# One decoder layer on one core: the order of the product stream worked out from product and wait lengths, with three groups' keys and values moved beside the first chain

## The chip, the cores and the metric

One core of a Trainium2 chip runs the whole layer in one launch. The metric is the time of an execution in microseconds of device time; the median of 3 runs of the kernel before is 2039.08 us (2031.9 to 2040.92).

## What is computed

The input x is 64 sequences of 128 tokens with 256 channels, the context ctx has the same shape, all in 32-bit floats. Cut to what matters:

```
x = layernorm(x + mamba(x))                  # xn = layernorm(x)*gamma+beta; xz = xn @ W_in (256 -> 2x512)
                                             # 4-tap causal convolution, silu, W_x -> B, C (16 each), delta
                                             # h = exp(delta*A)*h + delta*B*x ; y = h.C ; (y + D*x)*silu(z) @ W_out + x
x = layernorm(x + xattn(x, ctx))             # q = rot(x@Wq), k = rot(ctx@Wk), v = ctx@Wv ; (q k^T * decay) v, no softmax
x = layernorm(x + shared(x) + top-2 of 8 routed experts)   # silu(x@gate)*(x@up) @ down, hidden 512
```

`A` is the same for all channels here, so the kernel takes the branch `shared_decay`, which turns the recurrence into products of 128 x 128 matrices.

## The kernel before, in words

The 64 sequences are worked in 16 groups of 4 (512 tokens). A group goes through a **first half** (`front`, `scan`: layernorm, W_in, convolution, W_x, delta, the scan as products), a **second half** (`after`, `route`: W_out, layernorm, keys, values and queries, attention, layernorm, the router, and two scatters of 4 row blocks each to the expert lists in DRAM), and the **shared expert** (`shared`). Beside these run the **routed tiles**: 78 tiles of 256 or 128 rows, read from the lists, put through one expert's gate, up and down products with weights that are fetched tile by tile (1.5 MB each, three buffers), and scattered back. The tiles come in five batches; `tile_list` makes a batch's list after groups 4, 8, 12 and 16 (the last makes two).

Everything is written as Python generators that yield between steps. Each engine executes its instructions in the program's order, so the order in which the steps are recorded decides what a late operand holds up. Before, `weave` sets that order: for every yield of the first half of group g (30 are assumed) it advances the second half of group g-1 by 28/30 of a step, the shared expert of group g-2 by 8/30, and the routed tiles by 6 steps for each tile due in this tick; at the tick's end the others are run to their end. A tick is thus a border: nothing of tick g+1 stands ahead of what is left of tick g. The build then moves instructions locally on an engine where the build's own scheduling finds a gap, so the listing of the built program decides, not the source alone.

Names that the steps below use, by line of the kernel before: the normalised rows are transposed (L560, `xn` for the first half, `x` for the second), W_in makes `xc` and `sz` (L574), W_x (L630), `bcs` is transposed (L642), from it comes `dl` on VectorE and ScalarE (L673 to L694), the product of `d` (L713), 16 small products into `pof` (L724), `eb`, `bj`, `cj` (L729 to L731) and their product (L746), transposes of `xc` (L756), the product with `mt` (L763), W_out (L583), attention products (L837, L850), the router's `logit` (L909) and `sel` (L942). PSUM has 5 buffers `pm` and 3 `gu`; `cT`, the transposed context of one group, has one buffer and is loaded from the POOL queue. `one` is a pool of single buffers, so `sz` of the next group may be written only after W_out has read it.

After the 16 groups the rest of the tiles run with the shared expert of group 15 (L583/L574 on `gu`), then the shared experts of groups 7 to 13 beside the final sums (`combine`, L1208), layernorms and stores.

Of the kernel before, what the change touches and what calls it, by code (L numbers as in the profile page):

```python
# [11 lines left out]
F32 = mybir.dt.float32  # L12
# [497 lines left out]
def _shared_decay(ctx, K):  # L510
# [22 lines left out]

    xts = [K.x0] + [const.tile([P, GB, D], F32, name=f"xt{i}") for i in range(2)]

    def layernorm(dst, src):
# [12 lines left out]
        yield  # L549
# [5 lines left out]
    def transposed(dst, src, scale=None, bias=None):  # L555

        for k in range(KD):
            ps = pm.tile([P, T], F32, name="pm")
            for b in range(GB):
                nc.tensor.transpose(ps[:, b * L : (b + 1) * L], src[:, b, k * P : (k + 1) * P], ident)  # L560
            if scale is None:
                nc.scalar.copy(dst[:, k, :], ps)
            else:
                nc.scalar.activation(
                    dst[:, k, :], ps, AF.Identity, bias=bias[:, k : k + 1], scale=scale[:, k : k + 1]
                )
# [4 lines left out]
    def project(ps, w, col, src):  # L571

        for k in range(KD):
            nc.tensor.matmul(  # L574
                ps, lhsT=w[:, k, col : col + P], rhs=src[:, k, :],
                start=(k == 0), stop=(k == KD - 1),
            )

    def project_rows(ps, src, w, cols):

        chunks = len(src)
        for k in range(chunks):
            nc.tensor.matmul(ps, lhsT=src[k], rhs=w[:, k, cols], start=(k == 0), stop=(k == chunks - 1))  # L583
# [6 lines left out]
    def front(st):  # L590
# [5 lines left out]
        yield  # L596
        xnT = one.tile([P, KD, T], F32, name="xnT", tag="xnT")
        transposed(xnT, xn, gam, bet)
        yield
# [3 lines left out]
        for c in range(CI):  # L603
# [12 lines left out]
            yield  # L616
        nc.scalar.activation(xcf, xcf, AF.Silu)
        sz = one.tile([P, CI, T], F32, name="sz")
        for c in range(CI):
# [3 lines left out]
            yield  # L623
# [4 lines left out]
        for c in range(CI):  # L628
            for h in range(2):
                nc.tensor.matmul(  # L630
# [8 lines left out]
        yield  # L639
        ptk = pm.tile([P, 2, 2, 64], F32, name="pm")  # L640
        for j in range(2):
            nc.tensor.transpose(  # L642
# [26 lines left out]
        yield  # L669
# [7 lines left out]
        yield  # L677
# [11 lines left out]
        yield  # L689
# [5 lines left out]
        yield  # L695
        st.update(xcf=xcf, sz=sz, dl=dl, tok=tok, bj=bj, cj=cj, cq=cq)

    def scan(st):
# [11 lines left out]
        yield  # L710
        yield
        pin = pm.tile([P, GB, Q], F32, name="pm")
        nc.tensor.matmul(pin.rearrange("p b i -> p (b i)"), lhsT=after_in, rhs=d1.rearrange("p b i -> p (b i)"), start=True, stop=True)  # L713
# [5 lines left out]
        nc.scalar.activation(eq, eq, AF.Exp)  # L719
        yield  # L720
        pof = pm.tile([KB, T], F32, name="pm")
        for b in range(GB):
            for q in range(4):
                nc.tensor.matmul(  # L724
# [4 lines left out]
        nc.scalar.activation(eb, pof, AF.Exp, scale=a_col)  # L729
        nc.vector.tensor_tensor(bj, bj, eb, ALU.mult)  # L730
        nc.vector.tensor_tensor(cj, cj, eb, ALU.mult)  # L731
        yield
# [11 lines left out]
        pmt = pm.tile([P, GB, L], F32, name="pm")  # L744
        for b in range(GB):
            nc.tensor.matmul(  # L746
                pmt[:, b, :], lhsT=bj[:, b * L : (b + 1) * L], rhs=cj[:, b * L : (b + 1) * L], start=True, stop=True
            )
# [4 lines left out]
        for b in range(GB):  # L753
            ps = pm.tile([P, DI], F32, name="pm")
            for c in range(CI):
                nc.tensor.transpose(ps[:, c * P : (c + 1) * P], xcf[:, c, b * L : (b + 1) * L], ident)  # L756
            nc.scalar.activation(xd[b // 2][:, b % 2, :], ps, AF.Copy, scale=dl[:, b : b + 1])
            yield
        acc = st["sz"]
        for c in range(CI):  # L760
            ps = pm.tile([P, GB, L], F32, name="pm")
            for b in range(GB):
                nc.tensor.matmul(  # L763
# [7 lines left out]
            yield  # L771
        st["acc"] = acc

    def after(g, st):
# [3 lines left out]
        cT = one.tile([P, KD, T], F32, name="cT", tag="cT")  # L778
        nc.gpsimd.dma_start(
            out=cT, in_=ctxT[:, g * T : (g + 1) * T].rearrange("(k p) t -> p k t", p=P)  # L780
        )
# [12 lines left out]
        yield  # L794
        yield from layernorm(x1, x1)
        yield
        x1T = one.tile([P, KD, T], F32, name="x1T")
        transposed(x1T, x1)
        yield

        def rotated(w, src, table, name, tag):

            ev = pm.tile([P, T], F32, name="pm")
            od = pm.tile([P, T], F32, name="pm")
            project(ev, w, 0, src)
            project(od, w, P, src)
            cos = rot_s[:, table, :].unsqueeze(1).to_broadcast([P, GB, L])
            sin = rot_s[:, table + 1, :].unsqueeze(1).to_broadcast([P, GB, L])
            r = one.tile([P, 2, T], F32, name=name, tag=tag)
            r0, r1 = seqs(r[:, 0, :]), seqs(r[:, 1, :])  # L810
            tmp = one.tile([P, GB, L], F32, name="tmp", tag="tmp")
            nc.vector.tensor_tensor(r0, seqs(ev), cos, ALU.mult)
            nc.vector.tensor_tensor(tmp, seqs(od), sin, ALU.mult)
            nc.vector.tensor_tensor(r0, r0, tmp, ALU.subtract)
            nc.vector.tensor_tensor(r1, seqs(od), cos, ALU.mult)
            nc.vector.tensor_tensor(tmp, seqs(ev), sin, ALU.mult)
            nc.vector.tensor_tensor(r1, r1, tmp, ALU.add)
            return r

        kh = rotated(wk_s, cT, 2, "kh", "kh")  # L820
        yield
        v = one.tile([P, GB, D], F32, name="v")
        for j in range(GB // 2):
            ps = pm.tile([P, 2, D], F32, name="pm")
            for i in range(2):
                b = 2 * j + i
                project_rows(
                    ps[:, i, :], [cT[:, k, b * L : (b + 1) * L] for k in range(KD)], wv_s, slice(0, D)
                )
            nc.scalar.copy(v[:, 2 * j : 2 * j + 2, :], ps)  # L830
        yield
        qh = rotated(wq_s, x1T, 0, "qh", "qh")
        yield
        pss = pm.tile([P, GB, L], F32, name="pm")
        for b in range(GB):
            for half in range(2):
                nc.tensor.matmul(  # L837
# [6 lines left out]
        yield  # L844
        x2 = x1
        for j in range(GB // 2):
            ps = pm.tile([P, 2, D], F32, name="pm")
            for i in range(2):
                b = 2 * j + i
                nc.tensor.matmul(ps[:, i, :], lhsT=sc[:, b, :], rhs=v[:, b, :], start=True, stop=True)  # L850
# [3 lines left out]
        yield  # L854
# [36 lines left out]
    def route(g, st):  # L891
# [3 lines left out]
        yield  # L895
# [3 lines left out]
        for k in range(KD):  # L899
            for b in range(GB):  # L900
                nc.tensor.matmul(
# [5 lines left out]
        yield  # L907
        pr = pm.tile([P, GB, 32], F32, name="pm")
        nc.tensor.transpose(pr.rearrange("p b e -> p (b e)"), logit, ident)  # L909
# [3 lines left out]
        yield  # L913
# [24 lines left out]
        yield  # L938
        yield
        pc = pm.tile([P, GB, NE], F32, name="pm")  # L940
        pcf = pc.rearrange("p b e -> p (b e)")
        nc.tensor.matmul(pcf, lhsT=upto, rhs=sel.rearrange("p b e -> p (b e)"), start=True, stop=False)  # L942
        nc.tensor.matmul(pcf, lhsT=ones, rhs=pre.rearrange("p b e -> p (b e)"), start=False, stop=True)
        yield
# [26 lines left out]
        yield  # L971
# [7 lines left out]
        yield  # L979
# [5 lines left out]
    def shared(x2, x2T, x2s):  # L985
# [5 lines left out]
        for c in range(CF):  # L991
# [8 lines left out]
            yield  # L1000
# [20 lines left out]
    def tile_list(k):  # L1021
# [7 lines left out]
        nc.tensor.matmul(pn, lhsT=ones, rhs=count, start=True, stop=True)  # L1029
# [52 lines left out]
    def fill_behind():  # L1082


        for j in range(2 * NE - 1):
# [13 lines left out]
            yield  # L1099
# [3 lines left out]
    def refill():  # L1103

        while fetched[0] < min(room[0], known[0]):
            ahead.append(fetch(fetched[0]))
            fetched[0] += 1

    fetched = [0]
# [25 lines left out]
    def routed():  # L1135

        def hidden(i, t):
            _, size = shape(i)  # L1140
            w = weights[i % NW]
            wg = w[:, 0:SZ].rearrange("p (k i) -> p k i", k=KD)
            wu = w[:, SZ : 2 * SZ].rearrange("p (k i) -> p k i", k=KD)
            ps = pm.tile([P, KD, size], F32, name="pm")
            for k in range(KD):
                for j in range(size // P):
                    nc.tensor.transpose(ps[:, k, j * P : (j + 1) * P], t[:, j, k * P : (k + 1) * P], ident)  # L1147
            tT = tiles.tile([P, KD, size], F32, name="rows_T", bufs=2)
            nc.scalar.copy(tT, ps)
            to = tiles.tile([P, size // P], mybir.dt.int32, name="to", bufs=3)  # L1150
            nc.gpsimd.tensor_copy(to, t[:, :, D])
            wt = tiles.tile([P, size // P], F32, name="wt", bufs=3)
            nc.gpsimd.tensor_copy(wt, t[:, :, D + 1])
            yield
            hid = []
            each = T // size
            for c0 in range(0, CF, each):
                psg = gu.tile([P, each, size], F32, name="gu")
                psu = gu.tile([P, each, size], F32, name="gu")
                for ps, w2 in ((psg, wg), (psu, wu)):  # L1160
                    for c in range(each):
                        project(ps[:, c, :], w2, (c0 + c) * P, tT)
                    yield
                hc = tiles.tile([P, each, size], F32, name="hid", bufs=4)
                nc.scalar.activation(hc, psg, AF.Silu)  # L1165
                nc.vector.tensor_tensor(hc, hc, psu, ALU.mult)  # L1166
                hid += [hc[:, c, :] for c in range(each)]
            return hid, to, wt

        def down(i, hid, to, wt):  # L1170
            _, size = shape(i)
            wd = weights[i % NW][:, 2 * SZ :].rearrange("p (c h) -> p c h", c=CF)
            ps = pm.tile([P, size // P, D], F32, name="pm")
            y = tiles.tile([P, size // P, D], F32, name="rows_out", bufs=2)
            for j in range(size // P):
                project_rows(ps[:, j, :], [h[:, j * P : (j + 1) * P] for h in hid], wd, slice(0, D))
            for j in range(size // P):
                nc.scalar.activation(y[:, j, :], ps[:, j, :], AF.Copy, scale=wt[:, j : j + 1])  # L1178
                s = nc.gpsimd.indirect_dma_start(  # L1179
                    out=ys, in_=y[:, j, :], in_offset=None,  # L1180
# [408 lines left out]
```

## Time and profile before

| what | value |
|---|---|
| median of 3 runs | 2039.08 us |
| the profiled execution, its own time | 2045.25 us |
| its span, first to last instruction | 2043.5 us |
| TensorE matmul busy, instructions | 1897.4 us, 9252 |
| VectorE, ScalarE, GpSimd busy | 985.8, 775.4, 459.6 us |
| mean DMA rate | 124 GB/s |
| mean granted TensorE clock | 0.984 |
| `ACT_TABLE_LOAD` in the trace | 110, 1.283 us each |

How to read it: a product of 32-bit floats stands in the trace as two matmul instructions, a transpose as one. Busy time of TensorE is the union of the instructions from their start to their modelled end, so short pauses between pipelined products do not show as idle time. "A <- B" with a number is time in which the engine stood idle, and the instruction that ended the wait. The windows give the busy time of each engine in a stretch of the span.

### The profile page before, as it was taken

What the parts mean: (1) busy time and instruction counts of PE and PEld (TensorE: products, weight loads), DVE (VectorE), ACT (ScalarE), POOL (GpSimd) and SP (SyncE); (2) the same over time, 40 slices, a digit from 0 to 9 for tenths busy, and PEclk for the clock granted to TensorE, in tenths of its full rate; (3) what the DMA queues carried; (4) which work ended last, traced back from release to release, by engine and by line L of the source; (5) the groups of instructions that cost most, each with busy time, mean ns of one, the idle gap of its engine ahead of it and who ended that gap; (6) DMA issues with size and microseconds to landing.
All of it is one profiled execution on the core that took longest, in us unless ns stands there. A gap on an engine that the chain in (4) does not pass through costs nothing.

```text
span 2043.5 us, 26128 instructions
## 1 busy us (share of the span) xinstructions
PE 1897.4 (93%) x9252; PEld 1389.6 (68%) x9252; DVE 985.8 (48%) x2398; ACT 775.4 (38%) x1261; POOL 459.6 (22%) x697
## 2 busy tenths in 40 slices
PE   4899999899999999999998999999989999999997
PEld 2655666575767676777676777777767888887554
DVE  3666676555666546454545454554431111112573
ACT  3365355244443435353535353525222122221331
POOL 3021221130312122222223131313132122221110
PEclk9899999999999999999999999999999999999998
DMA  4111121431422234243434343424244455853772
GB/s 145 27 54 44 42 64 52 147 96 35 132 70 87 90 130 136 84 139 120 138 114 139 105 147 111 124 96 164 88 136 170 145 203 178 312 200 114 247 274 68
DMA packets 100628, 253.59 MB, mean 124 GB/s; under 512 B 22824, under 2 KB 60328, under 8 KB 91528
## 3 DMA queue, kind: packets, MB, share of 16 engines
q1 hardware_dynamic: 77368, 196.56, 29.7%
q0 software_dynamic: 17616, 52.46, 7.4%
q10 hardware_dynamic: 5504, 2.81, 0.5%
q8 instruction: 75, 1.23, 0.2%
q14 instruction: 65, 0.53, 0.1%
HBM read 207.33 MB, written 58.60 MB: 130 GB/s over the span
## 4 chain that ended last, share of the span: by engine, by line
PE 71%; DVE 10%; DMA 6%; ACT 5%; issue 3%; POOL 2%; another core or an unknown queue 1%; SPq 0%; DVEq 0%; ACTq 0%; POOLq 0%
PE gu L574 25%; PE pm L583 17%; PE pm L574 14%; PE gu L583 4%; PE pm L763 3%; DMA cq<-chunks 2%; DMA routed_w<-in_ffn_dram 2%; PE pm L560 2%; PE pm L837 1%; PE pm L756 1%; DVE st L541 1%; POOL rstd L546 1%; PE pm L850 1%; PE pm L1147 1%; DVE gq L738 1%
## 5 line engine op out<-in xcount | busy, mean ns | idle before, releaser
L574 PE MATMUL gu<-rows_T,routed_w 128*128 128x256 f32 (+1 forms) x2496 | 511.8, 355 | 12.1 <-DMA routed_w<-in_ffn_dram 5.8
L574 PEld LDWEIGHTS gu<-rows_T,routed_w 128*128 128x128 f32 x2496 | 416.4, 191 | 77.0 <-issue 27.7
L583 PE MATMUL pm<-routed_w,hid 128*128 128x256 f32 x1080 | 251.5, 381 | 9.9 <-DVE hid L1166 9.9
L1166 DVE TENSOR_TENSOR hid<-hid,gu 128x512 f32<-128x512 f32 x135 | 92.5, 685 | 327.7 <-PE gu L574 306.4
L574 PE MATMUL pm<-xnT,w_in_s 128*128 128x512 f32 x512 | 242.9, 598 | 1.8 <-DVE halfT L1302 1.1
L574 PE MATMUL gu<-x2T,shared_w 128*128 128x512 f32 x512 | 233.4, 601 | 0.9 <-DVE hc L998 0.9
L583 PEld LDWEIGHTS pm<-routed_w,hid 128*128 128x128 f32 x1080 | 200.7, 190 | 44.5 <-DVE hid L1166 14.7
L1179 POOL DMA_INDIRECT ys<-rows_out,to x135 | 134.9, 999 | 345.7 <-ACT rows_out L1178 304.0
L1165 ACT ACTIVATE hid<-gu 128x512 f32<-128x512 f32 x135 | 80.5, 596 | 239.2 <-PE gu L574 203.4
L574 PEld LDWEIGHTS gu<-x2T,shared_w 128*128 128x128 f32 x512 | 95.3, 191 | 108.9 <-issue 101.5
L612 DVE SCALAR_TENSOR_TENSOR xc<-pm,cw,xc 128x508 f32<-128x508 f32 (+2 forms) x192 | 140.2, 740 | 58.4 <-ACT xc L607 55.4
L1178 ACT ACTIVATE rows_out<-pm,wt 128x256 f32<-128x256 f32 x135 | 57.8, 471 | 272.4 <-PE pm L583 240.6
L574 PEld LDWEIGHTS pm<-xnT,w_in_s 128*128 128x128 f32 x512 | 95.5, 192 | 83.1 <-issue 71.0
L546 POOL TENSOR_TENSOR rstd<-var,mhalf 128x4 f32<-128x4 f32 x64 | 69.2, 1081 | 325.8 <-DVE var L544 174.5
L583 PE MATMUL gu<-shared_w,hc 128*128 128x256 f32 x512 | 125.1, 394 | 14.5 <-DVE hc L998 7.8
L583 PEld LDWEIGHTS gu<-shared_w,hc 128*128 128x128 f32 x512 | 97.2, 196 | 36.0 <-DVE hc L998 12.8
L583 PE MATMUL pm<-w_out_s,sz 128*128 128x256 f32 x512 | 115.2, 380 | 1.8 <-DVE xc L767 1.0
L583 PEld LDWEIGHTS pm<-w_out_s,sz 128*128 128x128 f32 x512 | 96.1, 190 | 16.3 <-DVE sz L770 2.1
L767 DVE SCALAR_TENSOR_TENSOR xc<-xc,dsk,pm 128x512 f32<-128x512 f32 x64 | 46.9, 743 | 114.6 <-PE pm L763 51.7
L551 ACT ACTIVATE x<-x,shift,rstd 128x256 f32<-128x256 f32 x136 | 73.3, 592 | 58.2 <-DVE shift L548 58.2
L607 ACT ACTIVATE xc<-pm,cb,cw 128x512 f32<-128x512 f32 x64 | 49.5, 774 | 115.8 <-PE pm L574 115.8
L974 POOL DMA_INDIRECT xs<-x,index x64 | 65.2, 1019 | 122.7 <-issue 41.9
(234 smaller groups left out, 2499.9 us busy)
## 6 DMA issues: line engine op xcount, KB each, us to landing
routed_w<-in_ffn_dram SPq DMA_DIRECT2D x78, 1536.0 KB
picked<-ys SPq DMA_DIRECT2D x16, 1024.0 KB
rows_in<-xs SPq DMA_DIRECT2D x57, 258.0 KB
cT<-in_ctxT_dram POOLq DMA_DIRECT2D x16, 512.0 KB
cq<-chunks SPq DMA_DIRECT2D x16, 512.0 KB
x_rows<-x SPq DMA_DIRECT2D x16, 512.0 KB
xt<-in_x_dram POOLq DMA_DIRECT2D x10, 512.0 KB
xt<-x_rows SPq DMA_DIRECT2D x10, 512.0 KB
```

The lines of the kernel that those rows point to most:

```text
L546: nc.gpsimd.tensor_tensor(rstd, var, mhalf, ALU.pow)
L551: nc.scalar.activation(dst[:, b, :], src[:, b, :], AF.Identity, bias=shift[:, b : b + 1], scale=rstd[:, b : b + 1])
L574: nc.tensor.matmul(ps, lhsT=w[:, k, col : col + P], rhs=src[:, k, :], start=(k == 0), stop=(k == KD - 1),)
L583: nc.tensor.matmul(ps, lhsT=src[k], rhs=w[:, k, cols], start=(k == 0), stop=(k == chunks - 1))
L607: nc.scalar.activation(xcf[:, c, :], ps, AF.Identity, bias=cb[:, c : c + 1], scale=cw[:, c, TAPS - 1 : TAPS],)
L612: nc.vector.scalar_tensor_tensor(xc[:, c, :, s:], ps3[:, :, : L - s], cw[:, c, TAPS - 1 - s : TAPS - s], xc[:, c, :, s:], ALU.mult, ALU.add,)
L763: nc.tensor.matmul(ps[:, b, :], lhsT=xd[b // 2][:, b % 2, c * P : (c + 1) * P], rhs=mtf[:, b, :], start=True, stop=True)
L974: s = nc.gpsimd.indirect_dma_start(out=xs, in_=rows[k][:, b, :], in_offset=None, out_offset=bass.IndirectOffsetOnAxis(ap=index[:, b, k : k ...
L1165: nc.scalar.activation(hc, psg, AF.Silu)
L1166: nc.vector.tensor_tensor(hc, hc, psu, ALU.mult)
L1178: nc.scalar.activation(y[:, j, :], ps[:, j, :], AF.Copy, scale=wt[:, j : j + 1])
L1179: s = nc.gpsimd.indirect_dma_start(out=ys, in_=y[:, j, :], in_offset=None, out_offset=bass.IndirectOffsetOnAxis(ap=to[:, j : j + 1], axis=0),)
```

## The change

The generators now yield numbers. `product` and `turn` wrap each matmul and transpose and add an assumed length to a running count `work`; a yield's number is the assumed time until the chain's next product has its operands. `abreast` takes the place of `weave`: of the chains whose wait is over by `work`, it advances the one that is least far along; if none is ready, it sets `work` forward. `placed` gives each chain its place: group number plus the share of an assumed length (54 for a first half, 60 for a second, 23 for a shared expert, 11 for a tile).

```diff
+    def product(out, lhsT, rhs, **how):
...
+        work[0] += 2 * max(0.00084 * n, 0.11 if n > 64 else 0.06) / tiled
+        nc.tensor.matmul(out, lhsT=lhsT, rhs=rhs, **how)
...
-    def weave(main, steps, *others):
...
+    def abreast(*chains):
+        alive = [[gen, whole, 0.0, 0.0] for gen, whole in chains]
+        while any(c[1] for c in alive):
+            able = [c for c in alive if c[3] <= work[0]]
+            if not able:
+                work[0] = min(c[3] for c in alive)
+                continue
+            c = min(able, key=lambda c: c[2])
+            try:
+                c[2], wait = next(c[0])
...
+            c[3] = work[0] + wait
```

The borders between ticks go: first halves, second halves, shared experts and tiles are four chains that run through all groups, each held only by what it needs (`read`, `scanned`, `routed`, `added`; the tiles by a list and by 12.0 of assumed time after a fetch).

Keys and values leave `after` and become `keys`; for groups 0, 1 and 2 a fifth chain `early_keys` makes them at the start, those of groups 1 and 2 in weight buffers of the tiles that are not yet in use. Their context is loaded from the SP queue, not POOL's:

```diff
+    def early_keys(places):
+        for g, place in enumerate(places):
+            cT = load_context(g, nc.sync)
+            yield 10.0 if g == 0 else 4.0
+            yield from keys(states[g], cT, place)
...
+    abreast(
+        (placed(early_keys([None] + weights[1:]), 0.0, 40.0), True), (first_halves(), True), (second_halves(), True), (shared_ones(), True), (tiles_beside(), True),
+    )
```

From group 3 on, the keys are made while the layernorm after W_out runs, before the transposes of `x1`. In `scan`, the products into `pof` stand ahead of `eq`'s exponent, `eb`'s exponent ahead of it too, and the product of `bj` and `cj` ahead of the operations on `eq`. The two scatters of 4 rows each in `route` get a yield of 5.0 after each. `down` of a tile yields between its row blocks. After the groups, `other_tiles`, `fill_behind` and the shared expert of group 15 run under `abreast`, then the late shared experts and the sums. No arithmetic changes.

## Prediction
> **What bounds the kernel now.** I read the busy times first, then the windows tick by tick, then TensorE's waits, then the timeline. The page's first part and its clock:
>
> ```profile
> PE 1897.4 (93%) x9252; PEld 1389.6 (68%) x9252; DVE 985.8 (48%) x2398; ACT 775.4 (38%) x1261; POOL 459.6 (22%) x697
> ...
> PEclk9899999999999999999999999999999999999998
> ```
>
> TensorE is the only engine near full. The change removes no product: the listing of both programs by engine (it has no times) holds the same 5106 products and transposes. So it can win only what TensorE loses between them, and 93% hides part of that. In dense stretches one instruction starts 0.429 us after the last for 128x512, 0.216 for 128x256, 0.112 for 128x128, 0.109 for a transpose; a product is two of these. Summed over the listing that is 1817 us. The span is 2043.5, so **226 us** are lost, not the 146 that the busy row leaves.
>
> Where: I cut the span at the first W_out product of each group (66.0, 139, 211.2 us ... in the timeline), one window per tick (columns: length, then busy us of PE, PEld, DVE, ACT, POOL, clock, DMA share, GB/s):
>
> ```profile
> 0.00:66.00 66.00, 34.91 (x152) 21.78 (x153) 29.07 (x82) 25.12 (x37) 17.12 (x58) 0.87 0.40 117
> 66.00:139.00 73.00, 67.25 (x310) 39.92 (x309) 49.10 (x120) 39.58 (x56) 10.52 (x11) 0.98 0.13 34
> ...
> 448.70:540.90 92.20, 91.62 (x442) 64.39 (x442) 55.75 (x128) 39.45 (x62) 21.23 (x25) 1.00 0.28 87
> ...
> 1037.60:1143.80 106.20, 96.54 (x484) 73.94 (x483) 55.61 (x146) 43.62 (x69) 25.30 (x35) 0.95 0.38 120
> 1143.80:1241.20 97.40, 93.44 (x482) 71.21 (x481) 51.69 (x123) 43.27 (x69) 25.92 (x35) 1.00 0.41 131
> ```
>
> Window length less the products' own time in it: tick 0 loses 66.0-24.1 = 41.9; ticks 1 to 4 together 33.7; 5 to 7 together 17.0; 8 and 12, in which a tile list is made, 10.7 and 15.6; the six other late ticks 46.5 (7.7 each: 98.1-90.4 and so on); from the last W_out to the last product 46; after the last product 14.6. These add to 226.
>
> What ends the waits:
>
> ```profile
> PE pm L713 <- DVE dlb L709: 16.8, 11, 2.7
> PE pm L746 <- DVE cj L731: 13.3, 8, 3.7
> PE pm L560 <- ACT xn L551: 10.7, 1, 10.7
> PE pm L583 <- DVE hid L1166: 9.9, 17, 0.6
> PE gu L583 <- DVE hc L998: 7.8, 7, 2.6
> PE pm L763 <- ACT xd L757: 7.3, 5, 5.0
> PE pm L713 <- DVE d L705: 6.6, 2, 4.9
> PE gu L583 <- DVE hid L1166: 6.2, 1, 6.2
> ```
>
> Two small chains off TensorE, the one to `dl` and the one to `cj`, make most of what recurs. That is what an order by lengths can move.
>
> **Tick 0: keys beside the first chain.** Three groups' keys and values are 3 x (4 x 0.858 + 8 x 0.432) = 20.6 us of products, and tick 0 has 41.9 us of loss, of which some 15 lie before x is normalised. They don't fit for free, since the listing puts them ahead of products that the chain waits for:
>
> ```profile
> 39.05 1.95 PE L630 MATMUL pm<-xc,w_x_s 128*64 128x256 f32 x16 [1.61 <-ACT xc L617]
> ...
> 41.47 0.44 PE L642 MATMUL pm<-ident,bcs 128*128 128x128 f32 x2 [0.47 <-ACT bcs L635]
> 41.94 0.30 DVE L646 COPY tok<-pm 128x132 f32<-128x132 f32 x1 [4.95 <-PE pm L642]
> ...
> 46.68 0.22 DVE L709 COPY dlb<-dl 128x128 f32<-128x128 f32 x1
> ```
>
> The 12 W_in products from 26.5 us on (10.3) plus group 0's 6.9 end at 43.7, where W_x started at 39.05: 4.6 late. Group 1's key products stand between W_x and `bcs`: 3.4, less the 0.6 that the copy takes anyway, 2.8. Four of its six VectorE rotations (0.69 each) stand ahead of `tok`: 2.4 after overlap. Group 2's 6.9 fill the 3.7 before `cj` and overrun by 2.7. So the first W_out comes 12.5 late, at 78.5, and 20.6 us are done: **-8**. The SP queue now holds the context loads ahead of `bcs`'s rows; the second waits until group 0's values have read the only `cT`, which is before W_x in TensorE's order, so nothing queued on SP behind it is late. Without that cover it would delay W_x's rows by a load, 2 to 4 us. POOL loses three issues of 0.7; nobody waits for it there.
>
> **Ticks 1 to 4.** The keys are gone from 1 and 2, but tick 1 then has only 50.7 us of products against a chain of about 58 (W_out 6.9, layernorm to its first block 4.0, transposes and queries, convolution 8.4 and silu 1.9 on VectorE and ScalarE, then `dl` 5, `cj` 5.6, the product with `mt` 3.6). So part of what is moved becomes idle time there. I take 33.7 to 26: **-8**.
>
> **The recurring waits, ticks 9 to 11 and 13 to 15.** I compare what a chain needs in the trace of before with the products that the listing of after leaves for it. `bcs` to `dlb`: 10.9 us in these ticks, with 8.8 of products beside it; alone, in tick 0, 5.0. VectorE did the router's `pb`, `gt`, `same` between its links; in after's listing nothing stands between them, and only two layernorm blocks (0.59 each) on ScalarE, so it needs about 6.2 and gets 7.8: -1.6 a tick. `d` to `cj`: needed 10.5 before; after it is 5.6 (tick 0) plus what ScalarE's copies add, against 5.3 of products and the 0.9 of `pof`: -1.0. `xd` -0.8, tile products that wait for an issue and PSUM -1.4. New waits: `sel` came 6.5 us of products before `cj` and now comes 6.5 to 7.8 after it, behind 9.4 us of VectorE work (eq's four operations 5.0, gt to rank 2.0, the rest): +1.7 over today's 0.5. The second layernorm's first block needs 4.8 after L850 and gets 4.1: +0.8. `logit` +0.4. Together -1.9 a tick, **-11** for six.
>
> **Ticks 5 to 7**: the first tile's rows (3.7) and weights (1.7) are waited for in 5; the 12.0 of assumed time covers that: **-5**. **Ticks 8 and 12**: TensorE stood 5.0 and 4.1 before L763, because `xd` sat on ScalarE behind a `rows_out` whose buffer waits for GpSimd, which was issuing 8 scatters. After's listing leaves 3.8 to 5.2 of products there, and both ticks show a clock below 1 (0.97 and 0.95), which comes back with the waits: **-10** of 26.3.
>
> The skill's page "TensorE: Matmul & The Clock Gate" (section "Why this matters for your kernels") says to avoid pauses over some 3 us, since the clock is then halved. The trace agrees: among these ticks only those with waits of 4 us and more show less than 0.99. By that rule the 2 us waits that I expect cost only themselves.
>
> **After the groups.** 6.2 us before L583 at 1500 go, because 16 of group 15's gate products (13.7 us) now stand where the last lists are fetched: **-6**. From the fifth tile after that to the end, the listing of TensorE is the same in both, so 40 us and the 14.6 behind the last product stay. ScalarE loads 89 tables instead of 110 (21 x 1.283 = 27 us of an engine that is 38% busy): nothing by itself, it is in the chains above.
>
> **Sum**: -8-8-11-5-10-6 = -48 on the execution of 2045.25: 1997. It lies 6.2 above the median of 2039.08, so on that scale **1991**.
>
> **Rivals.**
> (1) *The chains keep their lengths and the closer order meets them late: slower.* The place is `bcs` to `cj` in every late tick. If `dlb` still takes 10.9 and gets 7.8, and `cj` 10.5 and gets 6.2, with `sel` and the layernorm as above, a tick loses 3.1+4.3+2.5+0.8 = 10.7 and some 2 of small waits, 5 more than today; in 11 ticks +55, less the 22 of the start and the end, about +20 with some given back in ticks 8 and 12: 2058. It decides from about 2 us above my 6.2 and 5.9 in both chains. For it: those are the measured lengths. Against: the listing has VectorE's chain in one piece.
> The same page (table at its head) gives VectorE, ScalarE and GpSimd strict FIFO queues, which speaks against packing more chains: one late operation holds all behind it. The trace has such a case (`xd` behind `rows_out` above); the rule has no price.
> (2) *The waits only change places*: ticks 5 to 15 lose what they lose today, and only start and end win: -22, 2017.
> (3) *The plan holds*: no wait recurs, as ticks 6 and 7 show already (2.5 us each). Ticks 1 to 15 then lose 3 each, 45 for 123: -78, with -14 of start and end: 1947.
>
> **Numbers.** Forecast 0.45, (1) 0.17, (2) 0.26, (3) 0.12. What a measurement of this kernel tells from no change is about 0.5%, 10 us. Of the forecast all is faster; of (2), which spreads by 12 either way, 0.18 of 0.26 is faster and 0.06 the same; of (1) 0.14 is slower and 0.03 the same; with 0.01 of doubt about the rest: faster 0.75, same 0.10, slower 0.15. The range goes from (3) to the lower half of (1): 1947 to 2040.
>
> **What would show it.** First W_out at 76 to 80, second at 134 to 139; L713's waits under 5 us in all and L746's under 8; L942's waits up from 5 to 15 or more; no wait over 3 us before L763; ticks of 94 to 97 us late; TensorE's last 14 us as before. Wrong if L713 still waits 1 us and more in each tick (1), or if the first W_out comes after 85, where the early keys cost more than they carry.

## The result, and the profile after

| | before | after | ratio, 95% interval |
|---|---|---|---|
| median | 2039.08 us (17 runs, 2031.9 to 2045.65) | 2046.15 us (17 runs, 2037.98 to 2054.11) | 1.0036 (1.002 to 1.0051) |
| the profiled execution's span | 2043.5 us | 2050.0 us | |

The change gained nothing: the time is 0.4% longer, below the 0.5% that counts here, where 48 us less were forecast. A second set of runs of the same kernel gave 1.005 (1.0034 to 1.0067).

The page of the changed kernel, as of before: busy times, and the granted clock in 40 slices.

```profile
PE 1900.6 (93%) x9252; PEld 1397.3 (68%) x9252; DVE 987.6 (48%) x2398; ACT 745.7 (36%) x1240; POOL 457.6 (22%) x694
...
PEclk9999999999999999999999999999999999999998
```

ScalarE did 30 us less (89 table loads for 110), TensorE the same: none of it reached the end. Windows again from one first W_out to the next (length, then busy us of PE, PEld, DVE, ACT, POOL, clock, DMA share, GB/s):

```profile
0.00:80.30 80.30, 54.35 (x225) 32.37 (x226) 40.23 (x99) 28.08 (x43) 16.63 (x58) 0.94 0.41 116
80.30:141.20 60.90, 55.65 (x275) 33.33 (x274) 41.76 (x109) 32.51 (x49) 6.37 (x6) 0.97 0.11 28
...
449.60:539.90 90.30, 89.34 (x446) 64.88 (x445) 54.15 (x125) 38.47 (x61) 18.73 (x24) 1.00 0.27 85
...
1033.60:1124.20 90.60, 85.53 (x448) 64.91 (x448) 50.73 (x120) 39.36 (x65) 20.24 (x24) 1.00 0.28 90
1124.20:1233.90 109.70, 99.17 (x512) 76.12 (x511) 55.79 (x148) 41.51 (x69) 30.66 (x46) 1.00 0.46 157
```

The first tick is 14 us longer and the second 12 shorter, which is the early keys. Without borders the work of a late tick varies (448 matmul instructions in one of the lines above, 512 in the next), so lengths alone no longer compare. I therefore take, for every matmul instruction, the time to the next one's start less the median spacing of its kind, and add that up as the loss (without the 4.6 us ahead of the first product and the 14.6 behind the last, which are the same in both):

| loss in us | before | predicted | after |
|---|---|---|---|
| tick 0 | 36.5 | -8 | 29.8 |
| ticks 1 to 4 | 32.2 | -8 | 35.8 |
| ticks 5 to 7 | 15.6 | -5 | 12.9 |
| ticks 8 to 15 | 69.1 | -21 | 68.4 |
| from the last W_out to the last product | 44.7 | -6 | 55.1 |
| sum | 198 | -48 | 202 |

The last product ends 6.5 us later (2028.9, 2035.4): 4 of it are loss by this count. The rest is in the medians, above all that of the 32 instructions for `d` (0.131 us before, 0.205 after), which the count takes for their spacing.

What ends TensorE's waits now (in all, times, longest); `hid` L1211 (9.9) and `xn` (10.7) stand as before, `hc` rose from 8.7 to 11.3:

```profile
PE gu L543 <- ACT rows_T L1194: 16.5, 16, 3.3
PE gu L543 <- ACT hid L1210: 11.6, 7, 1.8
PE gu L543 <- DVE hc L1044: 11.3, 10, 1.9
PE gu L543 <- DMA routed_w<-in_ffn_dram: 11.2, 7, 3.6
...
PE pm L543 <- DVE sz L784: 9.7, 10, 1.9
PE pm L543 <- DVE mk L996: 9.3, 6, 3.0
...
PE pm L543 <- DVE cj L745: 5.4, 2, 3.3
PE pm L543 <- DVE dlb L725: 4.9, 3, 4.5
```

The waits that the change was to remove are gone: `dlb` 16.8 to 4.9 (4.5 of it in tick 0), `cj` 13.3 to 5.4, `d` 6.6 to 0.2, `xd` 7.3 to 0. In their place stand three that were 0.7 us or nothing, a tile's `rows_T`, its `hid` (through the `gu` buffers) and `sz` ahead of W_out, and a longer one for the router's choice (`mk`, 3.2 before).

### The profile page after: what moved, and what is told of

The parts are those of the page before. It is cut to its first block, busy times and chain, and to the rows that moved or that the text cites. A ratio compares the mean times of both kernels' runs of the same rounds, so it can differ in the third digit from the quotient of the medians.

```text
span 2050.0 us, 26104 instructions
## 1 busy us (share of the span) xinstructions
PE 1900.6 (93%) x9252; PEld 1397.3 (68%) x9252; DVE 987.6 (48%) x2398; ACT 745.7 (36%) x1240; POOL 457.6 (22%) x694
## 5 line engine op out<-in xcount | busy, mean ns | idle before, releaser
L543 PE MATMUL gu<-rows_T,routed_w 128*128 128x256 f32 (+1 forms) x2496 | 509.1, 357 | 39.8 <-ACT rows_T L1194 16.5
L1211 DVE TENSOR_TENSOR hid<-hid,gu 128x512 f32<-128x512 f32 x135 | 92.3, 686 | 388.1 <-PE gu L543 370.2
L543 PE MATMUL pm<-routed_w,hid 128*128 128x256 f32 x1080 | 258.4, 383 | 9.9 <-DVE hid L1211 9.9
L543 PE MATMUL pm<-w_out_s,sz 128*128 128x256 f32 x512 | 124.7, 396 | 10.5 <-DVE sz L784 9.7
L543 PE MATMUL gu<-shared_w,hc 128*128 128x256 f32 x512 | 116.9, 381 | 7.3 <-DVE hc L1044 7.3
L543 PEld LDWEIGHTS gu<-shared_w,hc 128*128 128x128 f32 x512 | 95.7, 190 | 28.1 <-DVE hc L1044 11.1
L781 DVE SCALAR_TENSOR_TENSOR xc<-xc,dsk,pm 128x512 f32<-128x512 f32 x64 | 47.0, 743 | 83.3 <-PE pm L543 56.1
```

The lines of the kernel that those rows point to most:

```text
L543: nc.tensor.matmul(out, lhsT=lhsT, rhs=rhs, **how)
L781: nc.vector.scalar_tensor_tensor(y, xcf[:, c, :], dsk[:, c : c + 1], ps.rearrange("p b l -> p (b l)"), ALU.mult, ALU.add)
```

## The experiments

My theory A: the assumed waits are lengths of idle engines. ScalarE and VectorE work through their queues in order and are 36% and 48% busy, so under load an operand comes 1 to 3 us later than assumed, and a closer order makes the next consumer wait. Rivals: B, the queues set the loss whatever the order; C, the loss is made at the start and in the tail; E, the late ticks have too few independent products, so a wait that is taken from one consumer comes up at another. Ratios are to the kernel before of the same set of runs, since one kernel differed by up to 1.5% between sets; the changed kernel itself has 1.0036 and 1.005. Even the ratio of one kernel moved by 0.7% between two sets (0.9951 and 1.0021, four tiles of empty rows below), so ratios of different sets compare only to about that.

**All assumed waits times 0.33, and times 2.**

```diff
-            yield at + span * min(1.0, passed / length), wait
+            yield at + span * min(1.0, passed / length), 0.33 * wait     # the other run: 2.0 * wait
```

> The changed kernel with every assumed wait cut to a third of itself, so that a chain comes back three times too early in the order. Theory A (the order follows the assumed waits, and these are lengths of idle engines, too short under load): shorter ones make each consumer wait longer, TensorE loses 3 to 6 us more in each of 15 ticks; 2046 becomes 2090 to 2130. Rival B (the waits do not matter, since the loss is set by the in-order queues of ScalarE and VectorE, whatever the order): 2036 to 2056. Rival C (the loss sits in the start and the tail): 2040 to 2055.

Measured: 1.0113 (1.0064 to 1.0162).

> The changed kernel with every assumed wait doubled. Theory A: the consumers that now wait (rows_T 16.5 us in all, hid 11.6, sz 9.7, the router's choice 9.3, x 6.6) find their data there, and independent products fill in; 25 to 35 us go, though at some places no independent product is left: 2012 to 2030. Rival B (queues set the loss): 2036 to 2056, the same waits under other names. Rival C (start and tail): 2040 to 2055.

Measured: 1.02 (1.0152 to 1.0248). So the lengths matter, against B, but a common factor is no cure, and A's numbers were missed both times: less was lost than it said in the first run, and the second went the other way. Doubled, TensorE ran out of fill in the ticks that have no tiles: 9.8 to 10.5 us for `dlb` in each of ticks 1 to 3 (33.5 in all), 19 and 23 us lost in ticks 8 and 12. The long chains' waits were not too short; which were, is the question.

**Without the early keys.**

```diff
-        (placed(early_keys([None] + weights[1:]), 0.0, 40.0), True), (first_halves(), True), ...
+        (first_halves(), True), ...
```

> The changed kernel without the early keys and values: each group's stand again in its own second half. Theory A gives the early keys what the trace shows, 20.6 us of products in a first tick that grew by 14.3: without them 2046 becomes 2050 to 2056, and the first W_out comes at 66 to 69. Rival D (the early keys cost more than they carry, since they lengthen the first chain and empty ticks 1 to 4 of products): 2030 to 2042, with ticks 1 to 4 losing 25 us and less in place of 36.

Measured: 1.0023 (1.0 to 1.0045), not to be told from the changed kernel. The first W_out comes at 67.3 in place of 80.3, the fourth at 278.6 in place of 280.9. Tick 0 loses 37.5 (29.8 with the keys), ticks 1 to 4 25.8 (35.8): what the early keys win in the first tick, the next four give back, as theory D has it; the net is about nothing.

**The last tile of the fourth list held back.**

```diff
+    per_tick[NG] -= 1
```

> The changed kernel with the last tile of the fourth list held back until the fifth list is made, so that its products run while the first tiles of that list are fetched. Theory A with the tail as its largest single part: TensorE's waits for routed weights between 1540 and 1600 (9 us) and the cold clock behind them go, the group 15 tick loses 2 to 4 us more for want of a tile: 2046 becomes 2034 to 2041. Rival B: 2044 to 2052, as what the tail wins the tick before it loses.

Measured: 1.0028 (1.0008 to 1.0049), a miss. The first fetches are covered now (0.2 us of wait), but one later wait for weights is 12.8 us long: SP's issue of that fetch stands behind four writes of empty rows (7.7 us on SP), and these wait for GpSimd, which changes the row numbers (SP stands 19.2 us for it between 1540 and 1600).

**Longer waits only where TensorE waits.**

```diff
-        yield 1.2                     # behind a tile's transposes
+        yield 2.2
-                yield                 # behind each gate and up product
+                yield 0.0 if w2 is wg else 1.0
-            yield 0.5                 # behind the products with mt
+            yield 0.5 if c < CI - 1 else 2.4
-        yield 4.6                     # behind the router
+        yield 6.0
```

> The changed kernel with longer assumed waits only where TensorE now waits: 2.2 for 1.2 behind a tile's transposes, 1.0 for 0 behind each gate and up pair, 2.4 for 0.5 behind the last product with mt, 6.0 for 4.6 behind the router. Theory A (those waits are too short under load): rows_T, hid, sz and the router's choice wait 15 us in place of 47, and 20 to 28 us go: 2018 to 2030. Theory E (in the late ticks two chains and four tiles leave too few independent products, so that a wait taken from one consumer comes up at another): within 8 us of the changed kernel, the named waits smaller and others (dlb, cj, x) larger.

Measured: 0.9983 (0.9958 to 1.0008), half of it: 0.5% below the changed kernel. The last group's W_out comes at 1418.8 in place of 1440.4, and then one wait of 15.1 us for weights takes most of that back. The waits in this run:

```profile
PE gu L543 <- DMA routed_w<-in_ffn_dram: 17.3, 4, 15.1
PE pm L547 <- ACT logit L953: 15.2, 7, 2.4
...
PE pm L543 <- ACT xnT L580: 9.2, 6, 3.2
PE gu L543 <- ACT rows_T L1194: 8.0, 10, 1.2
```

ScalarE's `hid` is out of the list, `sz` is down to 1.3 and `rows_T` is halved, but the next short waits in line, `logit` (0.6 assumed) and `xnT` (1.2), now wait. This is E's picture, or A's with more lengths that are too short.

**The empty rows written from GpSimd's queue.**

```diff
-                s = nc.sync.dma_start(out=xs[row : row + P, :], in_=zeros)
+                s = nc.gpsimd.dma_start(out=xs[row : row + P, :], in_=zeros)
```

> The changed kernel with the seven writes of empty rows behind the lists issued from GpSimd's queue in place of SP's. Theory F (in the tail SP stands 2 us and more before each of them, until GpSimd has changed the row, and the fetch of a tile's weights stands behind it): the waits for routed_w between 1575 and 1700 (some 5 us with what follows them) go, the first one of 3.6 at 1553 stays: 2038 to 2043. Rival (the fetch is bound by the transfer, not by its place on SP): 2043 to 2049.

Measured: 1.0073 (1.0046 to 1.01): F falls, it is no better. TensorE's waits for weights after the last group are 12.6 us in three where the changed kernel has 9.1 in three. SP's queue alone was not the cause.

**The scan's order as before.** ScalarE's `exp` of `eq` ahead of `eb`'s, the product of `bj` and `cj` behind the operations on `eq`.

> The changed kernel with the scan's own order as before: ScalarE's exponential of eq ahead of eb's, the product of bj and cj behind VectorE's four operations on eq. Theory A as predicted (the chain to cj is shorter with eb first): L746's kind of wait, for cj, comes back with 1 to 2 us a tick, 2046 becomes 2055 to 2070. Theory E: the wait for cj grows but those behind it shrink; within 6 us of the changed kernel.

Measured: 1.0042 (1.002 to 1.0064): no difference from the changed kernel. This part of the change is worth nothing that can be measured, for or against.

**No logarithm's table.**

```diff
-        nc.scalar.activation(lg, up, AF.Ln)
+        nc.vector.tensor_scalar(lg, up, 0.6931472, -0.6931472, ALU.mult, ALU.add)
```

> The changed kernel with the logarithm of 1 + e left out: a straight line on VectorE stands in its place, so ScalarE loads no table for it (16 of 89 loads of 1.28 us). The order on TensorE is the same. Theory Q (a tile's first silu waits on ScalarE behind the three table loads of the chain to dl): the 2 us waits for hid in the late ticks fall under 0.7, and some of those for dlb go: 8 to 20 us, 2026 to 2038. Theory E (TensorE waits elsewhere for as much): 2040 to 2048.

What it is about is seen in the changed kernel's timeline of ScalarE (start, length): ahead of the tile's `hid` stand the chain to `dl` with its table loads and a layernorm's blocks, while TensorE works off 24 instructions of gate and up products and then stands:

```profile
1089.63 0.21 ACT L692 ACTIVATE e<-raw 128x4 f32<-128x4 f32 x1 [0.65 <-DVE raw L690]
1089.75 0.59 ACT L567 ACTIVATE x<-x,shift,rstd 128x256 f32<-128x256 f32 x1
1090.35 1.28 ACT L693 ACT_TABLE_LOAD   x1
...
1092.36 1.28 ACT L698 ACT_TABLE_LOAD   x1
...
1094.37 1.28 ACT L1210 ACT_TABLE_LOAD   x1
1095.66 0.60 ACT L1210 ACTIVATE hid<-gu 128x512 f32<-128x512 f32 x1
```

```profile
1089.04 5.45 PE L543 MATMUL gu<-rows_T,routed_w 128*128 128x256 f32 x24 [0.76 <-ACT rows_T L1194]
1096.31 0.92 PE L543 MATMUL gu<-rows_T,routed_w 128*128 128x256 f32 x3 [1.82 <-ACT hid L1210]
```

The 1.82 us recur in the late ticks. Measured without the logarithm's load: 1.0051 (1.0031 to 1.007), no gain. The waits for ScalarE's `hid` went from 11.6 to 1.9, as Q expected, and those for `rows_T` rose from 16.5:

```profile
PE gu L543 <- ACT rows_T L1194: 22.7, 15, 3.1
...
PE gu L543 <- ACT hid L1210: 1.9, 6, 0.3
```

A faster ScalarE, under an unchanged order (VectorE got 16 small operations in exchange), moved the wait to the next consumer.

**Four tiles of empty rows in turn.** In the tail GpSimd raises the row numbers of one tile of empty rows between its fifteen writes, and waits until the write before has been read (changed kernel, GpSimd; the bracket is its wait):

```profile
1554.23 0.22 POOL L1133 TENSOR_SCALAR zeros<-zeros 128x1 f32<-128x1 f32 x1 [4.67 <-DMA xs<-zeros,behind_i]
...
1559.02 0.21 POOL L1133 TENSOR_SCALAR zeros<-zeros 128x1 f32<-128x1 f32 x1 [3.01 <-DMA xs<-zeros,behind_i]
...
1564.36 0.17 POOL L1167 COPY rows_in<-what 1x3 int32<-1x3 int32 x1
```

The copy at 1564.36, with which a fetch begins, is behind them in GpSimd's queue.

```diff
+            empty = empties[j % 4]
-            if j:
+            if j >= 4:
-                    zeros[:, D : D + 1], zeros[:, D : D + 1], float(P), None, ALU.add
+                    empty[:, D : D + 1], empty[:, D : D + 1], float(4 * P), None, ALU.add
```

> The changed kernel with four tiles of empty rows used in turn for the fifteen writes behind the lists, in place of one whose row numbers GpSimd raises after each write has been read (six more operations of GpSimd). Theory G (in the tail each such write holds GpSimd for the 2 to 5 us of the write before it, and GpSimd's copy that a tile's fetch begins with, and its scatters, stand behind it): TensorE's waits for routed_w after 1560 go, the first of 3.6 stays; 6 to 10 us: 2036 to 2041. Rival (the transfers themselves are slow there): 2043 to 2049.

Measured: 0.9951 (0.9934 to 0.9968). There the kernel before took 2021.47 us. Later, beside the changed kernel:

> The changed kernel with the four tiles of empty rows, now beside the changed kernel itself. Theory G (GpSimd's stand before each of the fifteen writes is what the changed order exposed in the tail): 8 to 16 us below the changed kernel, 0.995 to 0.999 of before. If it is within 4 us, the gain seen earlier was the chip's.

> The changed kernel as it is, on one chip with the three that follow, since chips differ by 1% (the kernel before took 2039 on two and 2021 on a third). Both theories: 1.002 to 1.005 of before.

Measured: 1.0021 (1.0004 to 1.0037) beside 1.005 (1.0034 to 1.0067). So in this set the four tiles are worth 0.3% to the changed kernel, by intervals that touch, and not the 0.85% that 0.9951 seemed to say beside 1.0036. That the chip was the reason, as the expectation has it, does not hold: the set with 2021 us and this one, with 2039.75 for the kernel before, carry the same chip number.

> The kernel before with the four tiles of empty rows. Theory G: its tail has only one wait for routed_w, 1.6 us at 1553, and two for rows_in of some 1 us, so 1 to 3 us go: 2036 to 2039 where the kernel before has 2039. If it gains as much as the changed kernel does, the tail is no part of the difference between the two.

Measured: 1.0011 (0.9992 to 1.003): no gain that can be told from nothing. If the 0.3% (6 us) of the changed kernel holds, it is a cost that the new order brought into the tail, a small part of the 55 us between forecast and result.

**Both, and three more waits longer.**

> The longer waits of the earlier run (2.2 behind a tile's transposes, 1.0 behind gate and up, 2.4 before W_out, 6.0 behind the router) together with the four tiles of empty rows. Theory A and G: that run stood 15.1 us for one routed_w in its tail, with a cold clock for 2 us behind it; both go, 2036 becomes 2016 to 2022. Rival to G: 2030 to 2037.

Measured: 0.9972 (0.9951 to 0.9993), a miss: in the same set of runs it is no better than the four tiles alone. `logit` still waits 15.1 us and `xnT` 8.5.

```diff
-        yield 0.6                     # ahead of logit's transpose
+        yield 2.8
-        yield 1.2                     # behind xnT
+        yield 2.4
-        yield 6.0                     # behind the router
+        yield 7.5
```

> The kernel of the run before this one with three more waits longer: 2.8 for 0.6 before logit's transpose (TensorE now waits 15.2 us there in all), 2.4 for 1.2 behind xnT (9.2), 7.5 for 6.0 behind the router (6.8). Theory A (there is still independent work, only the lengths are wrong): a further 12 to 20 us, 1999 to 2008. Theory E (the products that could stand there are used up): within 6 us of the run before it, the waits under other names.

Measured: 0.9794 (0.9756 to 0.9832), 34 us below the run before it (2016.91 to 1982.77) where A had 12 to 20. This decides between A and E: the products that could fill were there. Two windows of a tick each, shifted against W_out:

```profile
868.50:964.70 96.20, 95.68 (x495) 73.61 (x494) 52.63 (x124) 42.56 (x70) 26.02 (x35) 1.00 0.41 133
964.70:1060.00 95.30, 94.77 (x492) 73.01 (x491) 52.37 (x123) 42.51 (x70) 24.91 (x34) 1.00 0.41 134
```

0.5 us of idle TensorE in each. By the loss of the table, ticks 10, 11, 12 and 14 lose 1.7 to 1.8 each (6.0 to 11.4 in the changed kernel), ticks 8 to 15 24.7 for 68.4.

> All the longer waits (rows_T, gate and up, W_out, router, logit, xnT) with one tile of empty rows, as in the changed kernel. Theory A (most of the loss were lengths of idle engines): ticks 8 to 15 lose 25 to 32 us in place of 68, the tail keeps its 52 to 57: 0.984 to 0.990 of before. Theory G alone: without the four tiles nothing is left of the gain, 0.997 and more.

Measured: 0.9852 (0.9825 to 0.9879), in the set of runs in which the changed kernel had 1.005: the waits alone are worth 2.0% by the ratios (1.8% by the medians, 2049.45 to 2012.11 us). Its ticks 8 to 15 lose 37.4, and its tail has one wait of 13.2 us for weights.

> Four tiles of empty rows, and of the longer waits only those for logit (2.8), xnT (2.4) and the router (7.5); rows_T, gate and up and W_out keep theirs. Theory A in its strict form (each consumer that is left with a short wait stands for what the others were spared): rows_T, hid and sz still wait 25 us and more, 0.990 to 0.996 of before. If it comes under 0.983, logit's length alone was the fault, and the first round of longer waits did nothing.

Measured: 0.9941 (0.9922 to 0.996), 0.8% below the changed kernel with four tiles. `hid` still waits 11.5 us, `rows_T` 11.1. As A's strict form has it: the lengths that are left short spend part of what the others save.

> All the longer waits and the four tiles of empty rows (0.979 of before on an earlier chip), without the early keys and values. Theory H (the early keys fill the first tick and leave ticks 1 to 4 without products to stand beside their chains, so they carry little under any order): within 6 us of the same kernel with them, 0.976 to 0.983. If they carry what was predicted (8 us in tick 0 and nothing back): 0.983 to 0.988.

Measured: 0.9798 (0.9769 to 0.9828). In the time nothing can be told: the kernel with the early keys ran in another set (0.9794), or in this one with a tile held as well (1993.49 beside 2000.49 us). The traces speak against H, though. Without the early keys the fifth W_out comes at 358.1 us; with them, in this order, at 349.9 to 354.3, and ticks 0 to 4 lose 4 to 8 us less. In the changed kernel it was the other way (353.2 without, 355.4 with). So in the better order the early keys seem to carry much of the 8 us; each figure is from one execution.

> All the longer waits, the four tiles of empty rows, and the last tile of the fourth list held back until the fifth is made. Theory G and a second cause in the tail (no tile left while the new list's first rows and weights come; held back alone it met GpSimd's stand and a wait of 12.8 us): the wait for the first rows of the list, 5.6 us, goes and the group 15 tick loses 2 more: 0.974 to 0.979 of before. If the transfers bind, 0.979 to 0.984.

Measured: 0.9779 (0.9747 to 0.9812), 1993.49 us, the fastest of the study; not to be told from the kernel with no tile held (0.9794), but its tail is the shortest, 33.1 us of loss for 39.9 and, in the changed kernel, 55.1. The 200 us behind the last group, changed kernel and this one:

```profile
1440.40:1640.00 199.60, 184.25 (x784) 142.28 (x783) 52.25 (x143) 41.22 (x77) 46.47 (x82) 0.97 0.36 126
```

```profile
1399.10:1600.00 200.90, 198.63 (x894) 158.22 (x894) 51.18 (x142) 46.87 (x88) 53.01 (x95) 1.00 0.43 147
```

## Why the prediction was wrong, step by step

- **What bounds the kernel**: right. TensorE's losses are what an order can move, and the better orders moved 40 and more us of them.
- **Tick 0**, -8: right. The first W_out came at 80.3 (78.5 forecast), the loss fell by 6.7.
- **Ticks 1 to 4**, 33.7 to 26: wrong, 35.8. I let a part of the moved keys become idle time there; the run without them shows that in this order all of what tick 0 won is lost again: 25.8 without, 35.8 with. That 25.8 meets the forecast of 26 is luck: it is the order's own doing, and the keys' absence had to be added to it.
- **The recurring waits and ticks 8 and 12**, -21: wrong, -0.7; this is the step that failed most. The waits that I named went, by what I said and more. The new ones I priced at `sel` 1.7, a layernorm 0.8, `logit` 0.4. In a late tick after, `rows_T` cost 1.4 and `hid` 1.8, `sz` up to 2.5, `mk` 1.1 and less, the layernorm 0.4, `logit` nothing. I compared the chains to `dl` and `cj` with the products left for them and did not do the same for each other consumer with a short assumed wait, above all a tile's. By ticks: 8, 9, 12 and 13 lose 7 to 8 us less in sum (the lists are now made at the borders to 9 and 13), so the -10 for the lists nearly came; 10 and 11 lose what they lost, since `rows_T` and `hid` took the place of `dlb` and `cj`; 14 and 15 lose 9 more, with `sz` late in both. Rival (2) named the mechanism ("the waits only change places"), at 2017 since it kept the start and the end as gains. Neither of the two signs that were to show the prediction wrong appeared, as both look only at the chains to `dlb` and `cj` and at the first W_out.
- **Ticks 5 to 7**, -5: measured -2.7; 9.4 of the 12.9 are in tick 7, `rows_T` and `cj`.
- **After the groups**, -6: wrong, +10.4. Group 15's gate products do stand where the list is fetched, but all tiles of the fourth list are done by then. So nothing covers the first rows and weights of the new one, and the 32 instructions behind the first wait take 8.8 us in place of 7.1:

```profile
1553.23 8.81 PE L543 MATMUL gu<-rows_T,routed_w 128*128 128x256 f32 x32 [3.60 <-DMA routed_w<-in_ffn_dram]
...
1585.34 7.15 PE L543 MATMUL gu<-rows_T,routed_w 128*128 128x256 f32 x32 [2.57 <-DMA routed_w<-in_ffn_dram]
```

The part that was to stay did stay: from 1601 us before and 1609 after, where the order of TensorE is the same to the end, 33 and 31 us are lost. GpSimd's stands are a second cause; in the same stretch it also stands 21.4 us for its own scatters of `ys`. Alone, each remedy did little (held back 1.0028, four tiles 1.0021). With the longer waits both count: the tail loses some 50 us with one tile of empty rows, 39.9 with four, 33.1 with the last tile held as well, and then the first 200 us behind the last group have no wait for rows or weights over 0.3 us.
- **The end**, 14.6: right.
- **"The 2 us waits cost only themselves"**: wrong, see below.
- Rival (1), chains that meet the closer order late at `dlb` and `cj`: did not happen, and the scan's old order changed nothing. That its 2058 lies nearest to the measured time is chance.
- Rival (3), 3 us lost a tick: not by this change, but its ticks were reached (1.8) once the waits were right.

Not settled: which of the six longer waits is worth how much. They do not simply add up: the three for `logit`, `xnT` and the router gain 0.8% without the others (0.9941 for 1.0021) and 1.8% with them (0.9794 for 0.9972), each compared within one set and with the four tiles of empty rows; there the first round of longer waits gained nothing by itself (0.9972 for 0.9951). None of the six was tried alone.

## What to carry to other kernels

An order worked out from lengths is as good as its shortest wait: measure every producer-to-consumer time in the loaded trace, the short copies too, since the one that is left at its idle length spends much of what the others were spared. When a wait is to go, list what each engine's queue serves next and price that as well. Work that is moved to fill a hole early must be missed nowhere: compare the ticks it leaves with their chains, and again when the order has become better.

## What was not expected of the hardware

Waits well under 3 us can cost clock. In tick 14 of the changed kernel TensorE stood 0.91 and 1.28 us before W_out's products:

```profile
1236.33 0.70 PE L543 MATMUL pm<-w_out_s,sz 128*128 128x256 f32 x2 [0.91 <-DVE sz L784]
1238.31 7.57 PE L543 MATMUL pm<-w_out_s,sz 128*128 128x256 f32 x26 [1.28 <-DVE sz L784]
```

The 26 instructions take 0.29 us each where 0.216 is usual, and the clock of 1233 to 1243 is 0.83. The prediction took from the Trainium skill, "TensorE: Matmul & The Clock Gate" (section "Why this matters for your kernels"), the advice to avoid pauses over some 3 us, and concluded that 2 us leave the clock alone; here the measurement decides against that. The same page (section "A second HAM failure mode: psum-queue depth-cycling") tells of a kernel whose clock swings with frequent short pauses, which fits the row.

The trace of before had it already, in tick 3, which the prediction did not compare: one wait of 2.4 us at 265, and behind it the clock is half.

```profile
PE pm L713 <- DVE dlb L709: 2.4, 1, 2.4
```

```profile
266.50:269.50 3.00, 3.00 (x6) 1.79 (x6) 2.20 (x5) 2.34 (x2) 0.00 (x0) 0.50 0.01 3
```

Not every such wait does it: the 1.82 us for `hid` at 1096 stand in a window with clock 1.00 (1033.60 to 1124.20 above). Where the limit lies, no run here shows.

The same kernel with four tiles of empty rows took 2012.74 us in one set of runs and 2043.78 in another. Compared product by product, the second comes later in steps, among them 5 to 7 us around each of the W_outs of groups 12 to 15: ahead of them VectorE stood 2.1 us before its second L781 (at 1229.8 in tick 13), and not at all in the first set, with TensorE's instructions in the same order. TensorE waits 9.3 us for `sz` in the second set and 0.8 in the first. Beside the kernel before the same kernel is 0.5% faster in the first set and 0.2% slower in the second, so the sign of so small a difference hangs on something that these runs do not explain. Why is open.
